# Gate and up over the blend's four PSUM banks, silu and product over 1024 columns, and an order of issue from a clock of all engines

## The chip, the cores and the metric

The kernel runs on one core of a Trainium2 chip. The metric is the device time of one execution in microseconds (us). PE is TensorE, DVE VectorE, ACT ScalarE, POOL GpSimd, SP the engine whose queue issues most DMAs.

## The reference

Eight batches of 512 tokens with 256 channels pass through a block in four parts. In outline:

```python
y   = x[b] @ W[subject].T + bias[subject]                  # a matrix per batch
q, k = silu(y @ Wq), silu(y @ Wk); v = y @ Wv              # 16 heads of 16
q, k = rotated: concat(t*cos(theta*n), t*sin(theta*n))     # 32 per head
o   = (tril(q k^T)) v                                      # causal, no softmax
x1  = x + layernorm((o @ Wo) * sigmoid(y @ G1 @ G2)) * gamma + beta

ctx   = ema(x1)                                            # along the tokens
gated = x1 * sigmoid([x1, ctx] @ Wg + bg)
mod   = 0.5 + sigmoid(gelu(x1 @ Wn1 + bn1) @ Wn2 + bn2)    # 8 traces
temporal = sum_d softmax(blend)_d * ema_d(gated * mod_d)
c  = layernorm(gelu(x1 @ Wsoma + bsoma) * sigmoid(temporal @ Wtemp + btemp) @ Wout)

# feed-forward 256 -> 1024 -> 256, weights ternary, activations to 8 bits per token
h   = silu(quant(c) @ Wgate) * (quant(c) @ Wup)
out = x1 + quant(h) @ Wdown
```

## The kernel before

The work of a batch is cut into three generators: `attention(b)`, `cond2(b)` (everything from ctx to c) and `ffn(b)`. Two more, `setup_cond2` and `setup_ffn`, prepare the weights once. Each stops at `yield` and gives back the time from which its next piece is due. A planner at the end of the function keeps a number `now`, in microseconds, and at each step takes the piece of highest rank that is due: setup first, then feed-forward, then cond2, then attention. `now` is moved on by hand-written numbers: `spent(work, then)` adds `work` and answers `now + then`. So the order in which instructions are issued is fixed when the program is built; a framework beneath it may still put an instruction of the same engine a little earlier or later, and sets the semaphores.

The parts, by the names of their PSUM tiles, for token tiles t of 128 and channel halves k or o:

- attention: pxT (transposes of x), py (y), pkq and pv per tile (`project`), then per tile pkT and pqT (transposes of the rotated k and q) and pst (running states), pe (energies, masked into et on DVE), po (output, per two tiles), pg and pgt (gate), pw (Wo). The rotation, `ktok` and `qtok`, is one POOL instruction each. After pw come a gate product og, mean and variance, a power on POOL (`rstd_a`, for four tiles at once) and the sum into x.
- cond2: px2T, the scan cT, ph (h1), pso (soma), pm (mod), pwg (gated), pc and pr (what earlier chunks carry in), ptr (the traces within a chunk, in four banks at once, each followed by four accumulations into tempT on DVE, L765), ptg, pwo, then the norm c, its quantization to cq and a DMA transpose to cqT.
- ffn: `hidden(t)` makes the gate and up of a tile in halves of 512 columns, with silu (L861) and product (L862) for each half, then the maximum hmax, the scaling and the rounding to hq. A DMA transposes hq to hqT, pd is the down projection, res its sum with x, and a DMA stores it.

PSUM has eight banks of 512 float32 columns. Four are handed out singly from the pool `ps`; the other four are one tile of the pool `ps_t` (`four_banks`), which only the blend's ptr and the setup use. Gate and up take four single banks per token tile. The next attention begins when `tail[b]` is set, after `output(1)`.

```python
            hqs[t] = hq, hstep, spent(2.1, 6.0)

        hidden(0)
        yield now[0]
        for t in range(NT):
            if t + 1 < NT:
                hidden(t + 1)
            hq, hstep, at = hqs.pop(t)
            yield at
            hqT = p2.tile([P, KI, P], BF, tag="hqT", name=f"hqT_{b}_{t}")
            nc.sync.dma_start(hqT, hq, transpose=True)
            yield spent(0.0, 4.0)
```

Of the kernel before, what the change touches and what calls it, by code (L numbers as in the profile page):

```python
# [15 lines left out]
P = 128  # L16
EPS = 1e-5
# [13 lines left out]

@with_exitstack
def adaln_attn_ffn_kernel(ctx: ExitStack, tc: tile.TileContext, a: dict, out: bass.AP):
# [13 lines left out]
    cp = ctx.enter_context(tc.tile_pool(name="const", bufs=1))  # L47
    ps = ctx.enter_context(tc.tile_pool(name="ps", bufs=4, space=bass.MemoryType.PSUM))
    ps_t = ctx.enter_context(tc.tile_pool(name="ps_t", bufs=1, space=bass.MemoryType.PSUM))
    p1 = ctx.enter_context(tc.tile_pool(name="p1", bufs=1))  # L50
    p2 = ctx.enter_context(tc.tile_pool(name="p2", bufs=2))
    p3 = ctx.enter_context(tc.tile_pool(name="p3", bufs=3))
    p4 = ctx.enter_context(tc.tile_pool(name="p4", bufs=4))
    p6 = ctx.enter_context(tc.tile_pool(name="p6", bufs=6))
# [10 lines left out]
    now = [0.0]  # L65

    def spent(work, then):

        now[0] += work
        return now[0] + then  # L70
# [5 lines left out]
    nc.vector.tensor_copy(ident_bf, ident)  # L76
    ones = cp.tile([P, P], F32, name="ones")
    nc.vector.memset(ones, 1.0)
    minus_half = cp.tile([P, 1], F32, name="minus_half")
    nc.vector.memset(minus_half, -0.5)  # L80

    causal = cp.tile([P, 64], F32, name="causal")
    for r in range(2):
        nc.gpsimd.affine_select(
            out=causal[64 * r : 64 * (r + 1), :],
            in_=ones[64 * r : 64 * (r + 1), :64],
            pattern=[[1, 64]],
            compare_op=ALU.is_ge,
            fill=0.0,
            base=0,  # L90
            channel_multiplier=-1,
        )

    own = cp.tile([P, 2, 2, HD], F32, name="own")
    nc.vector.memset(own, 0.0)
    for j in range(4):
        nc.vector.memset(own[32 * j : 32 * (j + 1), j // 2, j % 2, :], 1.0)
# [3 lines left out]
    nc.sync.dma_start(sid_t, a["sid"].rearrange("(o n) -> o n", o=1))  # L101

    def load_input(b):
        xs = p4.tile([P, NT, C], F32, tag="x", name=f"x_{b}")
        nc.sync.dma_start(xs, x[b].rearrange("(t p) c -> p t c", p=P))
        sid = nc.sync.value_load(sid_t[0:1, b : b + 1], min_val=0, max_val=NS - 1)
        wt = p1.tile([P, KC, C], F32, tag="wt", name=f"wt_{b}")
        nc.sync.dma_start(
# [4 lines left out]
        nc.sync.dma_start(bt, a["biasT"][bass.ds(sid, 1)].rearrange("s p k -> (s p) k"))  # L113
# [5 lines left out]
    def load_w(name, src, eng=nc.sync):  # L119
        rows, cols = src.shape  # L120
        t = cp.tile([P, rows // P, cols], F32, name=name)
        eng.dma_start(t, src.rearrange("(k p) n -> p k n", p=P))
        return t

    def load_row(name, src):
        t = cp.tile([P, src.shape[0]], F32, name=name)
        nc.sync.dma_start(t, src.partition_broadcast(P))
# [3 lines left out]
    nc.scalar.dma_start(theta_c, a["theta_c"])  # L131

    wkq = cp.tile([P, KC, 2, C], F32, name="wkq")
    for i, n in enumerate(("wk", "wq")):
        nc.scalar.dma_start(wkq[:, :, i, :], a[n].rearrange("(k p) n -> p k n", p=P))
    wv = load_w("wv", a["wv"], eng=nc.scalar)
# [3 lines left out]
    nc.vector.memset(g1, 0.0)  # L140
    nc.sync.dma_start(g1[:, :, :HD], a["g1"].rearrange("(k p) n -> p k n", p=P))
    g2 = cp.tile([64, C], F32, name="g2")
    nc.vector.memset(g2, 0.0)
    for u in range(2):
        nc.sync.dma_start(g2[32 * u : 32 * u + HD, :], a["g2"])
# [6 lines left out]
    nc.sync.dma_start(tau, a["taus"].partition_broadcast(P))  # L152
    blend = p1.tile([D, C], F32, tag="blend", name="blend")
    nc.sync.dma_start(blend, a["blend"])
    raws = {}

    def load_raw(n, *places):
# [3 lines left out]
            pool.tile([P, half * cols], F32, tag=tag, name=f"{n}_raw_{s}") for s, (pool, tag) in enumerate(places)  # L161
        ]
        for s, raw in enumerate(raws[n]):
            nc.sync.dma_start(
# [10 lines left out]
    for s in range(2):  # L175
        nc.sync.dma_start(w["wn2"][HN * s : HN * (s + 1), :], a["wn2T"])
        nc.sync.dma_start(w["bn1"][HN * s : HN * (s + 1), :], a["bn1"].rearrange("(p o) -> p o", o=1))
    w["bn2"] = load_row("bn2", a["bn2"])
    for n in ("bsoma", "btemp"):
        w[n] = cp.tile([P, KC], F32, name=n)  # L180
        nc.sync.dma_start(w[n], a[n])
# [13 lines left out]
    for g in range(NG):  # L195
        nc.vector.tensor_scalar(diag[:, g, :], ident, theta_c[:, g : g + 1], None, ALU.mult)
    theta = bank("theta")
    nc.tensor.matmul(theta, ones, diag.rearrange("p g n -> p (g n)"), start=True, stop=True)
# [801 lines left out]
```

## Time and profile before

| | us |
|---|---|
| median of 3 runs | 779.91 |
| lowest, highest | 776.56, 782.77 |
| the profiled execution: its own time | 779.86 |
| the profiled execution: span in the profile | 778.2 |

The profile is of one execution. In a row of its groups stand line, engine, operation, output and inputs with shapes, count, then busy time in us, mean time of one in ns, and the idle time of the engine just before with what ended it. A row of the table by stage gives a stretch `from:to` and its length, then the busy time (and count of instructions) of PE, PE's weight loads (PEld), DVE, ACT and POOL, the granted TensorE clock, the DMA share and GB/s. A row of the timeline has start, length, engine, line and operation, and in brackets the idle time before it and who released it. In the rows of digits each digit is a fortieth of the span, in tenths. A float32 matmul shows as two records. The rows of the operations that the change touches:

| row | count | busy us | mean ns |
|---|---|---|---|
| silu, L861, 512 columns | 64 | 43.2 | 687 |
| product, L862, 512 columns | 64 | 45.9 | 744 |
| hmax, L864, 1024 columns | 32 | 38.9 | 1216 |
| ktok, L296 (POOL) | 32 | 41.2 | 1286 |
| blend accumulation, L765 | 128 | 95.8 | 748 |

### The profile page before, as it was taken

How to read it: one execution, taken by the hardware profiler on the slowest of the kernel's cores; microseconds unless marked ns; L12 is line 12 of the kernel's file. 1: busy time of each engine (PE TensorE's matmuls, PEld its weight loads, DVE VectorE, ACT ScalarE, POOL GpSimd, SP SyncE). 2: the span in 40 equal slices, each digit the busy share in tenths (PEclk: the TensorE clock that was granted, in tenths of full speed). 3: DMA queues.
4: the chain of work that ended last, by engine and by line, in shares of the span. 5: the costliest groups of instructions: out<-in, count | busy, mean ns of one | idle time of the engine just before them, and what ended most of it. 6: DMA issues, size and time to landing. Idle time of an engine off the chain costs nothing.

```text
span 778.2 us, 21224 instructions
## 1 busy us (share of the span) xinstructions
PE 665.8 (86%) x9330; PEld 445.2 (57%) x9330; DVE 505.7 (65%) x1047; ACT 260.5 (33%) x480; POOL 196.7 (25%) x223
## 2 busy tenths in 40 slices
PE   2988999799888999799888999799988999795644
PEld 1566666566664666566664666466764667454312
DVE  3896355785567665775658753776658755785565
ACT  2822343243224333253234332253234333240111
POOL 3542252114301251023311152113411252110000
PEclk7969999999999999899999999999999999898756
DMA  6700000021001210022001210021000200021011
GB/s 229 231 3 3 14 2 4 15 67 56 4 16 32 56 37 3 15 63 60 4 15 21 69 35 4 16 49 48 3 16 6 69 9 3 16 55 28 1 41 54
DMA packets 61198, 28.64 MB, mean 37 GB/s; under 512 B 46346, under 2 KB 60594, under 8 KB 61106
## 3 DMA queue, kind: packets, MB, share of 16 engines
q1 hardware_dynamic: 60146, 26.50, 12.8%
q8 instruction: 73, 1.20, 0.6%
q10 hardware_dynamic: 960, 0.79, 0.3%
q14 instruction: 19, 0.16, 0.1%
HBM read 12.60 MB, written 4.19 MB: 22 GB/s over the span
## 4 chain that ended last, share of the span: by engine, by line
PE 67%; DVE 18%; issue 5%; ACT 4%; DMA 3%; POOL 3%; ACTq 0%; POOLq 0%; DVEq 0%; SPq 0%
PE pkq L273 7%; PE pwg L710 7%; PE ptr L760 5%; PE po L375 5%; PE ptg L778 4%; PE pso L682 4%; PE pv L278 3%; PE pd L885 3%; PE pe L353 3%; PE pwo L803 3%; PE pst L316 3%; PE py L261 3%; PE pw L491 2%; PE pqT L303 2%; PE pkT L303 2%
## 5 line engine op out<-in xcount | busy, mean ns | idle before, releaser
L765 DVE SCALAR_TENSOR_TENSOR tempT<-ptr,bw_c,tempT 128x512 f32<-128x512 f32 x128 | 95.8, 748 | 41.8 <-PE ptr L760 39.1
L861 ACT ACTIVATE sig<-pw_gateT,steps 128x512 f32<-128x512 f32 x64 | 43.2, 687 | 80.5 <-PE pw_gateT L858 45.9
L296 POOL TENSOR_TENSOR ktok<-sg,cs 128x512 f32<-128x512 f32 x32 | 41.2, 1286 | 108.2 <-ACT sg L280 94.9
L858 PE MATMUL pw_gateT<-w_gateT,cqT 128*128 128x512 bf16 x128 | 40.3, 398 | 31.4 <-DVE h L862 24.7
L273 PE MATMUL pkq<-wkq,yT 128*128 128x512 f32 x128 | 64.2, 622 | 0.3 <-ACT yT L262 0.3
L858 PEld LDWEIGHTS <-cqT 128*128 128x128 bf16 x256 | 25.9, 101 | 64.6 <-issue 35.9
L862 DVE SCALAR_TENSOR_TENSOR h<-pw_upT,steps,sig 128x512 f32<-128x512 f32 x64 | 45.9, 744 | 15.2 <-ACT sig L861 8.8
L375 PE MATMUL po<-et,vz 64*32 64x64 f32 x2048 | 32.0, 246 | 25.0 <-DVE et L358 15.7
L327 POOL TENSOR_TENSOR st<-total,own 128x256 f32<-128x256 f32 x56 | 41.2, 752 | 48.1 <-DVE total L337 48.1
L760 PE MATMUL ptr<-dm,gated 32*128 32x128 f32 x1024 | 40.6, 293 | 10.7 <-DVE tempT L765 10.7
L358 DVE TENSOR_TENSOR et<-pe,causal 128x512 f32<-128x512 f32 x64 | 41.8, 685 | 12.2 <-PE pe L353 12.2
L296 POOL TENSOR_TENSOR qtok<-sg,cs 128x512 f32<-128x512 f32 x32 | 40.8, 1277 | 32.7 <-PE pst L316 32.5
L885 PE MATMUL pd<-w_downT,hqT 128*128 128x256 bf16 x256 | 35.9, 288 | 14.5 <-DMA hqT<-hq 14.5
L760 PEld LDWEIGHTS ptr<-dm,gated 32*128 32x128 f32 x1024 | 33.9, 194 | 21.5 <-issue 19.5
L375 PEld LDWEIGHTS po<-et,vz 64*32 64x32 f32 x2048 | 25.0, 114 | 32.4 <-DVE et L358 19.0
L353 PE MATMUL pe<-qT,kT 32*64 32x64 f32 x2048 | 41.6, 223 | 1.3 <-ACT qT L304 0.9
L858 PE MATMUL pw_upT<-w_upT,cqT 128*128 128x512 bf16 x128 | 41.5, 408 | 1.3 <-ACT sig L861 1.3
L353 PEld LDWEIGHTS pe<-qT,kT 32*64 32x64 f32 x2048 | 35.7, 135 | 10.9 <-issue 4.1
L887 DVE SCALAR_TENSOR_TENSOR res<-pd,hstep,x 128x256 f32<-128x256 f32 x32 | 15.4, 482 | 40.7 <-PE pd L885 40.7
L885 PEld LDWEIGHTS <-hqT 128*128 128x128 bf16 x256 | 25.8, 103 | 27.5 <-DMA hqT<-hq 19.4
L405 ACT COPY aT<-po 128x256 f32<-128x256 f32 x32 | 10.5, 375 | 91.6 <-PE po L375 91.6
L864 DVE TENSOR_REDUCE hmax<-h 128x1 f32<-128x1024 f32 x32 | 38.9, 1216 | 0.3
(201 smaller groups left out, 1338.6 us busy)
## 6 DMA issues: line engine op xcount, KB each, us to landing
x<-in_x_dram SPq DMA_DIRECT2D x8, 512.0 KB, 4.3
out_dram<-res SPq DMA_DIRECT2D x32, 128.0 KB, 1.7
wt<-in_weightT_dram SPq DMA_DIRECT2D x8, 256.0 KB, 2.8
w_gateT_raw<-in_w_gateT_dram SPq DMA_DIRECT2D x2, 512.0 KB, 6.7
w_upT_raw<-in_w_upT_dram SPq DMA_DIRECT2D x2, 512.0 KB, 7.9
w_downT_raw<-in_w_downT_dram SPq DMA_DIRECT2D x2, 512.0 KB, 7.5
wgT<-in_wgT_dram SPq DMA_DIRECT2D x1, 512.0 KB, 8.7
hqT<-hq SPq DMA_TRANSPOSE x32, 2.7
```

The lines of the kernel that those rows point to most:

```text
L273: nc.tensor.matmul(pkq, yT[:, k, chunk(t)], wkq[:, k].rearrange("p e c -> p (e c)"), start=k == 0, stop=k == KC - 1)
L296: nc.gpsimd.tensor_mul(tok.rearrange("p (h e d) -> p h e d", e=2, d=HD), sgs[t][:, i].unsqueeze(2).to_broadcast([P, H, 2, HD]), cs[:, t, : ...
L353: nc.tensor.matmul(pes[e][64 * r : 64 * (r + 1), g, u, :], kT[rows, g, at], qT[rows, g, at], start=True, stop=True)
L358: nc.vector.tensor_mul(et.rearrange("p g u n -> p (g u) n"), pes[e].rearrange("p g u n -> p (g u) n"), causal.unsqueeze(1).to_broadcast([P ...
L375: nc.tensor.matmul(po[r][q : q + 32, half, u, :], *factors, start=(r, q) not in begun, stop=last)
L710: nc.tensor.matmul(pwg[:, u, :], src[:, k % KC, chunk(t + u)], w["wgT"][:, k, :], start=k == 0, stop=k == 2 * KC - 1,)
L760: nc.tensor.matmul(ptr[:, r, :, t, :], gated[rows, t, chunk(k)], dm[rows, t], start=True, stop=True)
L765: nc.vector.scalar_tensor_tensor(acc, ptr[:, :, e].rearrange("p r t n -> p r (t n)"), w["bw_c"][:, k, d + e : d + e + 1], acc, ALU.mult, A ...
L858: nc.tensor.matmul(pm, cqT[:, t, k, :], w[n][:, k, cols], start=k == 0, stop=k == KC - 1)
L861: nc.scalar.activation(sig, pgu[0], AF.Silu, scale=steps[:, 0, t : t + 1])
L862: nc.vector.scalar_tensor_tensor(h[:, cols], pgu[1], steps[:, 1, t : t + 1], sig, ALU.mult, ALU.mult)
L885: nc.tensor.matmul(pd, hqT[:, k, :], w["w_downT"][:, k, :], start=k == 0, stop=k == KI - 1)
```

## The change

Three things change together.

**The feed-forward's tiles.** `hidden(t)` becomes `inner(t)`: gate and up of a token tile are written into one `four_banks` tile, gate in two banks and up in two; one silu and one product run over 1024 columns. `sig` is one buffer of 1024 instead of two of 512. The transpose to hqT is issued right behind hq.

**The order.** Each engine is wrapped, so that every instruction issued is also put on a `Clock`: it holds for each engine the time at which it is free, for each tile when its parts were last written and read, and for each pool when a buffer comes free. Its costs are fixed formulas by engine, operation and size (with numbers of its own for some groups of matmuls). On DVE, ACT, POOL and SP an instruction may be placed in an earlier gap. A generator no longer yields a time but a function, `needs(...)`, that says from the clock when tiles and a bank will be ready; the planner takes the piece of highest rank that is ready at PE's time. The ranks stay. Setup pieces are `paced` by DVE's time.

**Pieces cut and moved.** ktok and qtok are issued within `project` (with four buffers instead of three); the tile work after it, now `turned`, has a stop before each transpose. `output(0)` comes before the last tile's transposes. dm is made right behind modt. The norm after attention takes mean, variance and power per pair of tiles. The next attention may begin when `head[b]` is set, after pg, instead of `tail[b]`; some of its pieces wait for the previous attention's `tail` or its end. More stops are set between the parts of cond2.

```diff
+class Clock:
+    MATMULS = {"ptr": 0.069, "po": 0.028, "pg": 0.125, "pgt": 0.26, "pm": 0.26}
...
+        if engine == "vector":
+            if op in ("tensor_scalar", "tensor_copy", "memset"):
+                return 0.17 + 0.00062 * n
+            return (0.1 + 0.00217 * n) if op == "tensor_tensor_scan" else 0.13 + 0.00108 * n
+        if engine == "scalar":
...
+            return load + 0.165 + 0.0009 * n + (0.2 if "accum_out" in kw else 0.0)
...
+    def needs(*aps, banks=(ps, "ps"), when=lambda: True):
+        def ready():
+            return max([clock.when(v) for v in aps] + [banks[0].free(banks[1])]) if when() else None
+
+        return ready
...
-        r = p2.tile([P, NT], F32, tag="rstd", name=name)
+        r = p2.tile([P, 2], F32, tag="rstd", name=name)
...
+            for i, n in enumerate("kq"):
+
+                toks[t, i] = tok = p4.tile([P, NG * P], F32, tag="tok", name=f"{n}tok_{b}_{t}")
+                gp.tensor_mul(
...
+        def turned(t):
+
+            yield needs(toks[t, 0])
+            turn(t, 0)
+            states(t, toks[t, 0])
+            yield needs(toks[t, 1])
+            turn(t, 1)
...
+        head[b] = True
+        yield needs(kTs[1], qTs[1])
+        energies(1, 0)
...
-        def hidden(t):
+        def inner(t):
             h = p2.tile([P, INNER], F32, tag="h", name=f"h_{b}_{t}")
-            for j in range(INNER // 512):
-                cols = slice(j * 512, (j + 1) * 512)
-                pgu = []
-                for n in ("w_gateT", "w_upT"):
-                    pm = bank(f"p{n}_{b}_{t}_{j}")
+            yield needs(cqT[:, t], banks=(ps_t, "ptr"))
+
+            pgu = four_banks(f"pgu_{b}_{t}").rearrange("p (n j) m -> p n (j m)", n=2)
+            for i, n in enumerate(("w_gateT", "w_upT")):
+                for j in range(0, INNER, 512):
                     for k in range(KC):
-                        nc.tensor.matmul(pm, cqT[:, t, k, :], w[n][:, k, cols], start=k == 0, stop=k == KC - 1)
-                    pgu.append(pm)
-                sig = p2.tile([P, 512], F32, tag="sig", name=f"sig_{b}_{t}_{j}")
-                nc.scalar.activation(sig, pgu[0], AF.Silu, scale=steps[:, 0, t : t + 1])
-                nc.vector.scalar_tensor_tensor(h[:, cols], pgu[1], steps[:, 1, t : t + 1], sig, ALU.mult, ALU.mult)
+                        te.matmul(
+                            pgu[:, i, j : j + 512],
...
+            sig = p1.tile([P, INNER], F32, tag="sig", name=f"sig_{b}_{t}")
+            ac.activation(sig, pgu[:, 0], AF.Silu, scale=steps[:, 0, t : t + 1])
+            ve.scalar_tensor_tensor(h, pgu[:, 1], steps[:, 1, t : t + 1], sig, ALU.mult, ALU.mult)
...
+            hqT = p2.tile([P, KI, P], BF, tag="hqT", name=f"hqT_{b}_{t}")
+            sy.dma_start(hqT, hq, transpose=True)
+            hqs[t] = hqT, hstep
...
-        if b < B and b in loaded and tail[b - 1]:
+        if b < B and b in loaded and head[b - 1]:
...
-        ripe = [r for r in running if running[r][0] <= now[0]]
+        now = clock.at["tensor"]
+        ready = {r: v for r, v in ((r, running[r][0]()) for r in running) if v is not None}
+        ripe = [r for r in ready if ready[r] <= now]
```

In the prediction, pgu is the gate and up tile of the changed kernel.

## The prediction

> **What bounds the kernel now.** I read the page's busy shares first, then its 40 slices, then a table by stage, then the timeline of single gaps.
>
> ```profile
> PE 665.8 (86%) x9330; PEld 445.2 (57%) x9330; DVE 505.7 (65%) x1047; ACT 260.5 (33%) x480; POOL 196.7 (25%) x223
> PE   2988999799888999799888999799988999795644
> PEclk7969999999999999899999999999999999898756
> 240.70:328.69 87.99, 80.10 (x1166) 54.57 (x1165) 57.53 (x119) 30.38 (x57) 23.47 (x25) 0.97 0.12 32
> 666.42:778.20 111.78, 70.18 (x479) 40.68 (x478) 70.28 (x142) 23.06 (x40) 6.09 (x9) 0.77 0.13 33
> ```
>
> TensorE (PE) is nearly full everywhere except at both ends. Its dips come back every 88 us: one batch. The fourth line is one whole batch: 80.1 of 87.99 us busy, so 7.9 idle. Over the five batches from 152.29 to 592.00 the idle time is 8.3, 7.9, 8.6, 7.8 and 6.5. The last line is what follows the last attention: 41.6 of 111.8 us idle. Of the 112.4 us idle in all, some 49 lie in the middle (80 to 666), 42 at the end, 21 before 80. The gaps of one batch:
>
> ```profile
> 314.36 0.35 PE L375 MATMUL po<-et,vz 64*32 64x64 f32 x16 [1.93 <-DVE et L358]
> 324.88 1.28 DVE L506 SCALAR_TENSOR_TENSOR x<-og,rstd_a,x 128x256 f32<-128x256 f32 x3 [1.24 <-POOL rstd_a L244]
> 326.47 0.75 DVE L862 SCALAR_TENSOR_TENSOR h<-pw_upT,steps,sig 128x512 f32<-128x512 f32 x1
> 327.27 0.59 PE L858 MATMUL pw_gateT<-w_gateT,cqT 128*128 128x512 bf16 x2 [3.53 <-DVE h L862]
> 743.79 1.04 PE L858 MATMUL pw_gateT<-w_gateT,cqT 128*128 128x512 bf16 x2 [6.65 <-DMA cqT<-cq]
> 771.16 3.67 PE L885 MATMUL pd<-w_downT,hqT 128*128 128x256 bf16 x16 [6.72 <-DMA hqT<-hq]
> ```
>
> The 3.53 us gap is the bank shortage: the next gate needs one of four single banks, the banks wait for the product h, and h stands on VectorE (DVE) behind a whole layer norm that itself waits 1.24 us for GpSimd's power. The last two lines are the end: nothing is left to fill PE while the last feed-forward goes round through the transposes.
>
> [...] (a pair of gate matmuls takes 1.04 us after the 6.65 us gap, 0.59 otherwise); after the 3.53 us gap the pair takes 0.59, so in mid-kernel a gap costs itself and no more. [...]
>
> **The change part by part.**
>
> *Four banks, two at once.* Per token tile, two silus (2 x 0.687) become one of 1024. No row shows that; ScalarE's (ACT) Gelu takes 474 ns for 256 elements and 687 for 512, 0.83 ns an element, so 1.11 us (the 1024-wide Sin row says 1.14). Two products (2 x 0.744) become one: 482 for 256 and 744 for 512 give 1.27. Saved: 0.25 on ACT and 0.22 on DVE per tile, 8 and 7 us over 32 tiles. Neither engine bounds, so I book nothing for it alone. What matters is that gate and up leave the four single banks, so the 3.53 us gap as such goes. What is late next: the four-bank buffer exists once, for feed-forward and blend, so gate (t+1) and the first blend wait for product t. From the last up matmul that takes about 2.0 us on a free DVE: silu ends 0.2 + 1.11 after the gate, 0.87 earlier, then 1.27, then hops. sig's single buffer adds no other wait. In the changed order 3.0 to 4.5 us of other matmuls stand between two such tiles. More on DVE is worth more than on ACT.
>
> *Transposes.* hqT is issued behind its hq, no longer at a later step. On SP's queue an input load (wt, which waits for the y matmuls) stands before hqT of tile 0 in every other batch; those matmuls end about 1 us before hq does. Output stores stand before some later hqT but wait for a down projection already past. Booked at nothing; up to 1 us a batch if wrong.
>
> *Moved POOL work.* ktok and qtok (1.29 and 1.28 us) are issued with the projection, not at their transposes, removing the releaser "PE pst" (32.5 us in the waits); dm (1.04 each) goes up to modt. POOL is 25% busy. The layer norm's rstd is taken per pair of tiles: one pow of 0.70 and a small op of 0.19 twice instead of 1.04 + 0.37, so the first pair of x no longer waits for the last pair. At the end this takes about 2 us off the way to the last transposes of x2.
>
> *Tables.* Counted in ACT's order, switches between Gelu and Silu tables go from 17 to 23, 6 x 1.28 = 8 us of ACT at 33%. The one that is near the path is silu 0 in the batches where it falls between h1 and soma; 3.5 us of pso and 1.1 of pm cover it. Booked at nothing, bound 8 us.
>
> *The order.* The order really differs, and the steady state becomes a pair of batches: in one (A) the whole feed-forward stands beside the next attention's head, in the other (B) beside the blend's head. I walked both along PE's, DVE's and POOL's order with durations from the rows above (pkq 1.72 a tile, pv 0.87, pe 1.10 a half, ptr 1.10, pso and py 3.5 and so on; DVE back to back).
> - A, first gate: after pwo's first tile come square 0.57, c 0.69, rstd 0.9, and on to cq; in the trace 307.1 to 313.6, then 2.4 to land: 9.0 us. PE has only 6.1 us to do meanwhile (half a pe, pwo, pgt, pe, three quarters of pw). Wait 3.3.
> - A, first down projection: the norm's instructions stand among hmax to hq; hqT lands 1.3 us late.
> - A, last down projection: DVE has about 38 us of work in these 42 us; hqT of tile 3 lands 3.1 us late.
> - A's blend hands the buffer over with 2.1 and 3.2 us of cover against 3.0 of DVE: 1.5 us together.
> - B: down projection of tile 2 waits 2.7, the rest about 0.8.
>
> That is 13 us in two batches, 6.5 each: the gaps are mostly replaced, not removed. But the matmuls get shorter as well: today pw is threaded into the last po stream, 314.36 to 320.92 with 1.0 before it, which costs 1.8 us more than the two apart (2.6 + 3.5); clean, a batch is 77.5 us. So 77.5 + 6.5 = 84.0; as PE arrives 1.3 us later at these waits than my rounded durations had it, 83.4. Against (592.00 - 152.29)/5 = 87.9 that is 4.5 us a batch.
>
> *Both ends.* Until 80 us PE waits 5.6 us from 53 to 81 (masks behind weight setup, then the first layer norm). The next batch's transposes, y and two projections now stand in that norm: 3 us saved, between 0 and 6. At the end, the norm by pairs saves its 2 us, and the last feed-forward is DVE's chain, 4.9 us a tile: from cqT at zero, hq of the four tiles at 7.9, 12.1, 17.7 and 23.8 (two results res stand before an hq and wait about 1 us), then 2.8 + 1.7 + 0.6 + 3 to the end: 32 against 778.2 - 743.8 = 34.4. But all four tiles of batch 6 now lie beside the last blend's head, about 28 us of DVE against 25 us today, which takes back 2 to 3. Net 2 us.
>
> *Sum.* 4.5 us x 6.7 batches (80 to 672) = 30, and 3 + 2: 35 us off the span of 778.2, 743. Outside the span lie 779.86 - 778.2 = 1.7 us: 745. The profiled execution and the median of the runs (779.91) agree, so no correction.
>
> **The rivals.**
> - *Nearly full filling.* The walk has DVE strictly behind; if the waits shrink to 1.5 us a batch, it is 79 us, 8.9 x 6.7 + 5 = 65 off: 715. For it: DVE is 57.5 of 88 us busy on average. Against it: it is dense where the feed-forward is.
> - *The waits move and don't shrink.* As many gaps as today plus the DVE backlog, 8.5 us a batch: 86.0, 1.9 x 6.7 + 5 = 18 off: 762. If the threading of po and pw isn't won either, 775 to 780: the change then doesn't do what its order says. For it: the durations on which an order rests are fixed numbers in both kernels, and today's order leaves 8 us as well.
> - *Slower: the one four-bank buffer.* Five handovers a batch (four tiles, then the first blend). If DVE is behind at each by 1 us more than walked, 5 us a batch, the gain of 4.5 + 0.7 is gone; from there it decides. At 2 us more: (10 - 5.2) x 6.7 = 32 us slower, 812. For it: today DVE was 3.5 us behind at exactly such a product. Against: 3.0 to 4.5 us of cover at each, and DVE spared 0.22 us a tile.
>
> **How the numbers follow.** My forecast, 728 to 760, has 0.60; nearly full filling 0.13; moved waits (760 to 772) 0.11; within 1%, which is about what a measurement of this kernel can tell from no change, 0.08; slower 0.08. So faster by over 1% is 0.84. The range 716 to 777 leaves out half of the full filling and the slower end: under 2 in 10. The bounds of unknown terms are inside it: tables up to +8, SP up to +7, waits per batch 1.5 to 8.5.
>
> **What would show it.** Right: batches of about 83 us; no PE gap released by the product of 0.5 us or more except at the first gate; the longest mid-kernel PE gaps at the first gate (cqT) and at down projections (hqT), 1 to 3 us; the silu near 1.1, the product near 1.27; a last stage from the last cqT of 32 us. Wrong: gaps of over 2 us before gates or blends, released by DVE, in every batch (the buffer), or batches of 86 us and more, or of 80 and less.

## The result and the profile after

The changed kernel takes 784.07 us (median of 20 runs, 779.88 to 792.12), the kernel before 781.53 beside it (20 runs, 776.56 to 790.6): 1.0034 of before, 95% interval 1.001 to 1.0058. (Ratios leave out slow executions, over 1.5% above the fastest of the same kernel; medians count all.) The forecast was 745. The profiled execution of the changed kernel took 789.42 us (span 787.7), some 5 us above its own median, so the two traces lie 9.5 us apart where the medians lie 2.5 apart.

In the changed kernel nearly all instructions carry the line of the engine wrapper (L167), so groups are told apart by their tiles; pgu is gate and up. First the page's busy shares of PE and DVE, PE's slices and granted clock:

```profile
PE 661.9 (84%) x9313; PEld 443.1 (56%) x9330; DVE 511.4 (65%) x1015; ACT 254.0 (32%) x452; POOL 213.4 (27%) x239
...
PE   2789898889988899999898798999988899685654
...
PEclk7977899989999999999999999999999999896756
```

PE's dips are still there and the idle time has grown (125.8 us against 112.4). From the table by stage, a whole pair of batches twice (the order repeats every two), then what follows the last attention's output projection:

```profile
267.76:441.19 173.43, 157.35 (x2324) 107.47 (x2329) 116.95 (x231) 61.17 (x108) 51.40 (x54) 0.96 0.14 32
441.19:612.50 171.31, 154.77 (x2323) 105.75 (x2329) 116.87 (x231) 61.18 (x108) 51.39 (x54) 0.98 0.12 28
674.10:787.70 113.60, 67.01 (x354) 37.25 (x355) 70.08 (x139) 20.28 (x32) 6.73 (x11) 0.72 0.13 33
```

A batch takes (173.43 + 171.31)/4 = 86.2 us, of it 78.0 busy and 8.2 idle; before it took 87.9. The last row is 113.6 us long; before, from the same matmul to the end, it was 106. PE's waits over the whole run (us, times, longest), the kernel before:

```profile
PE pw_gateT L858 <- DVE h L862: 24.7, 7, 3.5
PE po L375 <- DVE et L358: 15.7, 9, 1.9
PE pd L885 <- DMA hqT<-hq: 14.5, 3, 6.7
```

and the changed kernel, then the same view of its pair 267.7 to 441.19 alone:

```profile
PE pd L167 <- DMA hqT<-hq: 19.9, 11, 4.4
PE pgu L167 <- DMA cqT<-cq: 19.9, 5, 6.7
...
PE pqT L167 <- DVE res L167: 11.3, 6, 2.7
PE pgu L167 <- DVE h L167: 7.6, 3, 2.5
```
```profile
PE pqT L167 <- DVE res L167: 6.4, 3, 2.7
PE pd L167 <- DMA hqT<-hq: 4.8, 2, 3.1
PE po L167 <- issue: 3.7, 2, 2.3
PE ptr L167 <- DVE tempT L167: 1.6, 3, 1.0
```

The wait of the gate for the product is gone from the middle, as forecast; its last three cases are in the last feed-forward, and the last blend waits 2.0 us for a product once (at 707.6). In its place stand many waits of 0.4 to 3 us. (Of the 6.4 us, 2.66 end just where the window begins.)

At the head, VectorE in the changed kernel, then before:

```profile
65.97 1.29 DVE L167 TENSOR_TENSOR et<-pe,causal 128x512 f32<-128x512 f32 x2 [1.25 <-PE pe L167]
75.35 0.16 DVE L167 TENSOR_SCALAR wstep<-pwsum 128x1 f32<-128x1 f32 x1 [8.10 <-PE pwsum L167]
...
75.75 1.42 DVE L167 TENSOR_SCALAR w_downT_raw<-w_downT_raw,winv 128x1024 f32<-128x1024 f32 x2
...
79.67 0.75 DVE L167 SCALAR_TENSOR_TENSOR og<-gate,pw 128x256 f32<-128x256 f32 x2
```
```profile
70.60 0.75 DVE L496 SCALAR_TENSOR_TENSOR og<-gate,pw 128x256 f32<-128x256 f32 x2 [5.06 <-issue]
```

VectorE stands 8.1 us for a sum over w_down (pwsum) that PE issues only behind the po stream, then does that weight's setup, and only then the first norm (og): 9 us later than before. The first blend's last ptg ends at 142.2 instead of 126.8. Not all of this belongs to the change. last_single (below) issues the same instructions in the same order up to the last batch; in its profiled execution og begins at 77.09 and that ptg ends at 137.7. The granted clock up to 160 us is 0.94 there and 0.88 here: the eight y matmuls that begin at 75.18 take 5.38 us here and 3.68 there. So about 4.5 of the 15 us (142.2 against 137.7), by my estimate from these two executions, go with the granted clock of this one.

At the end, PE's timeline:

```profile
750.54 0.61 PE L167 MATMUL pgu<-w_gateT,cqT 128*128 128x512 bf16 x1 [6.65 <-DMA cqT<-cq]
...
756.66 1.87 PE L167 MATMUL pgu<-w_gateT,cqT 128*128 128x512 bf16 x4 [2.52 <-DVE h L167]
...
762.75 1.86 PE L167 MATMUL pgu<-w_gateT,cqT 128*128 128x512 bf16 x4 [2.52 <-DVE h L167]
...
776.19 1.89 PE L167 MATMUL pd<-w_downT,hqT 128*128 128x256 bf16 x8 [2.41 <-DMA hqT<-hq]
782.49 1.89 PE L167 MATMUL pd<-w_downT,hqT 128*128 128x256 bf16 x8 [4.42 <-DMA hqT<-hq]
```

The gates start 6.1 to 6.8 us apart: eight matmuls, silu, product, in series on the one buffer. Of the 6.1 us from 756.66 to 762.75, the eight matmuls take 3.6, at a granted clock of 0.50, and the handover 2.52; from 750.5 to the end the granted clock is 0.59. From the last cqT to the end it takes 37.2 us; before it was 34.4.

### The profile page after: what moved, and what is told of

Same layout as the page of the kernel before. It is cut to its first block, busy times and chain, and to the rows that moved or that the text cites. A ratio compares the mean times of both kernels' runs of the same rounds, so it can differ in the third digit from the quotient of the medians.

```text
span 787.7 us, 21069 instructions
## 1 busy us (share of the span) xinstructions
PE 661.9 (84%) x9313; PEld 443.1 (56%) x9330; DVE 511.4 (65%) x1015; ACT 254.0 (32%) x452; POOL 213.4 (27%) x239
## 4 chain that ended last, share of the span: by engine, by line
PE 51%; DVE 16%; DMA 5%; issue 4%; ACT 3%; POOL 1%; POOLq 0%; DVEq 0%; ACTq 0%; SPq 0%
PE pgu L167 6%; PE pwg L167 6%; PE pkq L167 6%; DVE tempT L167 5%; PE ptr L167 4%; DMA hqT<-hq 3%; PE ptg L167 3%; PE pso L167 3%; PE pd L167 3%; PE pwo L167 3%; PE pv L167 2%; DVE h L167 2%; PE po L167 2%; DVE c L167 2%; PE pr L167 2%
## 5 line engine op out<-in xcount | busy, mean ns | idle before, releaser
L167 DVE SCALAR_TENSOR_TENSOR tempT<-ptr,bw_c,tempT 128x512 f32<-128x512 f32 x128 | 96.0, 750 | 36.4 <-PE ptr L167 33.1
L167 POOL TENSOR_TENSOR ktok<-sg,cs 128x512 f32<-128x512 f32 x32 | 41.3, 1292 | 171.1 <-ACT sg L167 157.7
L167 PE MATMUL pkq<-wkq,yT 128*128 128x512 f32 x128 | 71.0, 678 | 0.3 <-DMA bg<-in_bg_dram 0.3
L167 DVE SCALAR_TENSOR_TENSOR h<-pgu,steps,sig 128x1024 f32<-128x1024 f32 x32 | 41.0, 1280 | 42.6 <-ACT sig L167 42.6
L167 POOL TENSOR_TENSOR st<-total,own 128x256 f32<-128x256 f32 x56 | 44.5, 807 | 87.9 <-DVE total L167 87.4
L167 ACT ACTIVATE sig<-pgu,steps 128x1024 f32<-128x1024 f32 x32 | 35.7, 1115 | 90.4 <-PE pgu L167 90.4
L167 PEld LDWEIGHTS <-cqT 128*128 128x128 bf16 x256 | 26.0, 105 | 62.4 <-DMA cqT<-cq 22.2
L167 PE MATMUL pgu<-w_gateT,cqT 128*128 128x512 bf16 x111 | 35.2, 425 | 28.7 <-DMA cqT<-cq 19.9
L167 PE MATMUL ptr<-dm,gated 32*128 32x128 f32 x1024 | 44.0, 298 | 17.4 <-DVE tempT L167 15.2
L167 PE MATMUL pd<-w_downT,hqT 128*128 128x256 bf16 x256 | 37.6, 296 | 20.6 <-DMA hqT<-hq 19.9
L167 PEld LDWEIGHTS ptr<-dm,gated 32*128 32x128 f32 x1024 | 36.4, 198 | 28.5 <-issue 21.4
L167 DVE TENSOR_TENSOR et<-pe,causal 128x512 f32<-128x512 f32 x64 | 41.6, 681 | 7.2 <-PE pe L167 7.2
L167 POOL TENSOR_TENSOR qtok<-sg,cs 128x512 f32<-128x512 f32 x32 | 46.0, 1437 | 0.0
L167 PEld LDWEIGHTS <-hqT 128*128 128x128 bf16 x256 | 25.5, 105 | 31.7 <-DMA hqT<-hq 24.2
L167 PEld LDWEIGHTS pe<-qT,kT 32*64 32x64 f32 x2048 | 35.8, 136 | 12.3 <-issue 8.4
L167 PE MATMUL pe<-qT,kT 32*64 32x64 f32 x2048 | 41.4, 225 | 0.1
L167 ACT ACTIVATE sg<-pkq 128x512 f32<-128x512 f32 x32 | 19.1, 598 | 65.4 <-PE pkq L167 65.4
L167 ACT ACT_TABLE_LOAD x28 | 35.9, 1283 | 12.7 <-PE pkq L167 7.6
L167 DVE TENSOR_REDUCE hmax<-h 128x1 f32<-128x1024 f32 x32 | 38.7, 1210 | 0.3
L167 PE MATMUL py<-xT,wt 128*128 128x512 f32 x64 | 34.5, 673 | 3.6 <-ACT xT L167 3.6
L167 PE MATMUL pgu<-w_upT,cqT 128*128 128x512 bf16 x128 | 37.0, 415 | 0.0
L167 PEld LDWEIGHTS pkq<-wkq,yT 128*128 128x128 f32 x128 | 25.5, 217 | 20.3 <-issue 17.2
```

The lines of the kernel that those rows point to most:

```text
L167: made = issue(*args, **kw)
```

## The experiments

Ratios are to the kernel before, run beside each on the same chip, with their 95% intervals; the changed kernel's is 1.0034. The theories that the expectations name: 1, the middle's waits are VectorE's backlog, as the new order packs its work too densely; 2, the last feed-forward goes in series through the one buffer; 3, the pacing of the weight setup delays the first norm; 4, which batch of a pair comes last decides the end. Three more came up on the way: 5, the clock packs the feed-forward so closely that it uses up whatever VectorE is relieved of; 6, the clock's PE runs ahead of the chip's; 7, VectorE's instructions get longer beside GpSimd's. An order is "made anew" where the clock is told of an edit, and "kept" where it counts the old instruction.

### One half of the change at a time

banks_only: the kernel before, with (in outline)

```diff
-                for n in ("w_gateT", "w_upT"): pm = bank(...)     # two silus, two products
+            pgu = four_banks(f"pgu_{b}_{t}")                       # one silu, one product
```

> The kernel before with its own planner and order; gate and up go into the four-bank tile, one silu and one product over 1024 columns; no clock. Theory 1 (the new order packs VectorE's feed-forward and norm work too densely, and that is why 4 us a batch did not come): the buffer alone takes away the 3.5 us gap before a gate in each batch but adds handovers to the blend, and costs at the end, where a silu cannot start before the up matmuls are done (3 x 2 us): 772 to 785 us. Rival A (the buffer brings the gain and the new order gives it back): 750 to 765. Rival B (the buffer itself is the loss and the order the gain): 795 to 815, with waits of 2 us and more for the product before gates or blends in every batch.

order_only: the changed kernel, with the opposite edit in `inner`.

> The changed kernel's clock, order and moved pieces; gate and up in halves of 512 in four single banks, two silus and two products per tile, as before. Theory 1 (VectorE dense in the new order): the batch stays at 86 to 88 us, since VectorE has 0.2 us more per tile, and the end is 4 to 6 us shorter than in the changed kernel because silu follows its own half: 777 to 787 us. Rival B (the shared buffer is what holds the batch at 86): batches of 83, 755 to 765. Rival A (buffer gains, order loses): 800 and more.

Measured: banks_only 797.29 us, 1.0156 of before (1.01 to 1.0212); order_only 826.53, 1.0563 (1.052 to 1.0607). Both are slower than the two together. PE's waits, banks_only first, then order_only:

```profile
PE px2T L658 <- DVE x L506: 27.2, 9, 3.8
PE pd L888 <- DMA hqT<-hq: 21.4, 10, 4.4
```
```profile
PE pd L167 <- DMA hqT<-hq: 48.0, 10, 7.5
PE pw_gateT L167 <- DMA cqT<-cq: 34.0, 8, 7.0
```

With the old order the 3.5 us gap before a gate only moves on, to the transposes of x2 that wait for the norm: 24.7 us became 27.2. With the new order and single banks a batch takes 92 us. Neither came out as theory 1 had it: banks_only fell in the range of rival B, for which the buffer is the loss, and order_only in that of rival A, for which the order is. A reading that fits both is that the order needs the single banks that the buffer sets free, and the buffer needs the order. What is shown is that each half alone loses in the one form tried; in order_only the clock also made its order anew, and the order alone can move this kernel by tens of us (below).

### Where the next attention begins

```diff
-        if b < B and b in loaded and head[b - 1]:
+        if b < B and b in loaded and tail[b - 1]:
```

> The changed kernel, but the next attention begins where it did before the change, at the previous one's tail and not at its head. Theory (the early start is what makes the long and short batches alternate, and fills PE): batches of equal length, about 87 to 89 us, total 788 to 800. Rival (alternation is itself a loss, because in every second batch the whole feed-forward stands beside one other stage): batches of 83 to 85, total 765 to 775.

Measured: 791.4 us, 1.0107 (1.0072 to 1.0142), with batches of nearly equal length (84 to 91 us between the transposes of x2). The early start is a gain of 6 to 7 us, with the order that came with it.

### Head and end

setup_early, in `paced`:

```diff
-        return lambda: max([clock.when(v) for v in aps] + [clock.at["vector"] - 1.0])
+        return lambda: max([clock.when(v) for v in aps], default=0.0)
```

> The changed kernel, but the pieces of the weight setup come as soon as their inputs are there, not paced by VectorE's time. Theory 3 (pacing puts the weight setup of w_down between the first attention's output and its norm, and the first wpo ends 10 us later than before): first transposes of x2 back at 78 to 80 us instead of 87, total 6 to 9 us less, 775 to 778. Rival (PE has other work then, the next attention's head, so the time is not lost but taken later): total within 2 us of the changed kernel, with the following batch's stages no earlier than in it.

Measured: 773.41 us, 0.9872 (0.9828 to 0.9916). Its norm begins without the setup ahead of it:

```profile
72.74 0.75 DVE L167 SCALAR_TENSOR_TENSOR og<-gate,pw 128x256 f32<-128x256 f32 x2 [2.12 <-issue]
```

PE is idle 10.1 us from 30 to 160 instead of 18.5, and the first blend's last ptg ends at 130.0. But the edit also turned the pair over: the long intervals now follow the other batches, and from the last output projection to the end it takes 101 us, not 113.6, since less of batch 6's feed-forward lies beside the last blend. flip1 turns the pair over with the setup left paced:

```diff
-        if b < B and b in loaded and head[b - 1]:
+        if b < B and b in loaded and (tail if b == 1 else head)[b - 1]:
```

> The changed kernel, weight setup paced as in it; only the second attention (batch 1) begins at the tail of the first one, all later ones at the head as in the changed kernel. This turns the alternation over: the batches with the long interval become the odd ones, as in the run with unpaced setup, and the last blend no longer has the sixth batch's feed-forward beside it. Theory 4 (of the 11 us that unpaced setup won, the larger part is which batch comes last): 107 us from the last attention's output projection to the end become 100 to 103, and the total is 774 to 779. Rival (the setup's place itself is the loss): the end may be shorter, but the later start of batch 1 costs as much: 782 to 788.

Measured: 780.04 us, 0.9957 (0.9934 to 0.998). The end shortened to 104 us; the head was hardly better than in the changed kernel (16.5 us idle from 30 to 160). So, as far as one run of each can tell, roughly half of what setup_early won (0.8 of 1.6%) is which of the two batches comes last, and the other half is the head.

last_single: single banks in the last batch alone (`if b == B - 1:` with the old code).

> The changed kernel, only the last batch's gate and up in halves in four single banks. Theory 2 (at the end PE, silu and product go in series on the one four-bank buffer, 2.5 us of wait and a halved clock per tile): from the last cqT to the end 31 to 33 us instead of 37, total 4 to 6 us less than the changed kernel, 778 to 780. Rival (the end is VectorE's chain of about 5 us a tile, whatever the banks): 36 to 37 us, total within 1 us of the changed kernel or slower by 1 from VectorE's 0.2 us a tile.

Measured: 780.01 us, 0.9971 (0.9922 to 1.002): 4 us less than the changed kernel, though the two intervals touch. Its last feed-forward on PE:

```profile
746.17 0.63 PE L167 MATMUL pw_gateT<-w_gateT,cqT 128*128 128x512 bf16 x1 [7.05 <-DMA cqT<-cq]
...
771.78 3.34 PE L167 MATMUL pd<-w_downT,hqT 128*128 128x256 bf16 x16 [6.79 <-DMA hqT<-hq]
```

No gate waits for a product here, and from the last cqT to the end it takes 32.3 us instead of 37.2. That is the shortest of its kind. In the other traces with single banks at the end and the same work per tile it takes 34.4 (the kernel before), 34.6 (order_only), 34.9 (best) and 35.3 us (early_last); in those with the one buffer, 36.3 to 38.3. So the one buffer made the end longer, by about 3 us rather than 5. VectorE's chain counts at least as much: hmax_same and hmax_short (below), with the one buffer and one shorter VectorE instruction a tile, take 32.1 and 32.0 us.

> The changed kernel with both edits: weight setup not paced, and the last batch's gate and up in single banks. If head and end are independent losses they add up: 773.4 - 4 = 769. If what single banks saved was chance of order: 773 as without them. If the last feed-forward is then bound by VectorE: 771 to 773.

early_last, both edits: 772.66 us, 0.9814 (0.9767 to 0.9861). Its median is 0.8 us under that of setup_early, and the intervals of the two ratios overlap. That the two gains add up is not shown, and the 769 was not reached.

### VectorE's amount, or the chain of one tile

hmax_short and hmax_same shorten one VectorE instruction a tile:

```diff
-            ve.tensor_reduce(hmax, h, AX.X, ALU.max, apply_absolute_value=True)
+            ve.tensor_reduce(hmax, h[:, :8], AX.X, ALU.max, apply_absolute_value=True)      # hmax_short
+            nc.vector.tensor_reduce(hmax, h[:, :8], AX.X, ALU.max, ...)                     # hmax_same
+            clock.account("vector", "tensor_reduce", (hmax, h), {})
```

> The changed kernel, with the maximum of h taken over 8 of its 1024 columns (so the scaling of h, and the output, are other numbers): VectorE has about 1.0 us less per token tile, 4 us a batch, and nothing else moves in the chip; the clock counts the shorter instruction and may shift the order a little. Theory 1 (the waits at cqT, hqT, res and tempT are VectorE's backlog): a pair of batches takes 164 to 167 us instead of 172 to 173, the end is 4 us shorter, total 750 to 762. Rival (the waits are fixed latencies of transposes, hops and the order, VectorE's amount of work hardly matters): pair 170 and more, total 776 to 782.

> As hmax_short (maximum over 8 of 1024 columns, another scaling of h), but the clock counts the instruction at its full size, so the order of issue is the changed kernel's own to the last instruction: VectorE has about 1.0 us less per token tile and nothing else differs. Theory 1 (the middle's waits are VectorE's backlog; in hmax_short the clock used the time up by packing tiles closer): a pair of batches takes 164 to 168 us instead of 172, total 755 to 765. Rival (waits are set by fixed chains, not by VectorE's amount): pair 170 to 172, total 774 to 780.

Measured: hmax_short 778.82 us, 0.9954 (0.9927 to 0.9981); hmax_same 763.35, 0.9725 (0.9668 to 0.9782). The same relief of the chip is worth 21 us where the clock is not told of it and 5 where it is: with the shorter cost the clock makes another order. Between the second and the seventh transposes of x2, two batches take 174 to 175 us in hmax_short and 164 to 168 in hmax_same, against 166 to 174 in the changed kernel.

scale_act takes another VectorE instruction away and puts it on ScalarE, the clock not told:

```diff
-            ve.tensor_scalar(h, h, hinv, MAGIC, ALU.mult, ALU.add)
+            nc.scalar.activation(h, h, AF.Identity, bias=magic, scale=hinv)
+            clock.account("vector", "tensor_scalar", (h, h), {})
```

> The changed kernel, the scaling of h (0.75 us a tile on VectorE) done by ScalarE (about 1.1 us), with the clock still counting it on VectorE, so that the order stays. VectorE has 27 us less in all and the scaling no longer meets GpSimd; each tile's own chain gets about 0.5 us longer. Theory 1 (relief of VectorE pays where GpSimd doesn't get more): hmax_same won 0.65 us per us of VectorE taken away, so 12 to 18 us less, minus the longer chain at the end (2): 768 to 774. Rival (the single chain of a tile decides, not VectorE's total): 784 to 790.

Measured: 802.86 us, 1.0221 (1.0188 to 1.0254), 19 us slower than the changed kernel. VectorE is busy 489.7 us there, 484.5 in hmax_same, 511.4 in the changed kernel: it lost much the same work both times, with opposite results. What differs is the chain of one tile: from the end of the product to the end of hq it takes 4.07 us on average in the changed kernel, 2.81 in hmax_same, 4.96 in scale_act. PE's waits for hqT, 19.9 us in the changed kernel, follow it (hmax_same, then scale_act):

```profile
PE pd L167 <- DMA hqT<-hq: 10.4, 8, 3.3
```
```profile
PE pd L167 <- DMA hqT<-hq: 34.3, 11, 4.4
```

So theory 1 fell in the form it was given. With the changed kernel's order, it is the length of a tile's own chain that the middle pays for, not VectorE's total. Two things stay open: scale_act is slower than even the rival expected (784 to 790), and it makes ScalarE 36.7 us busier (290.7), which was not tested apart.

### res off VectorE, and GpSimd's part

res_on_act, and res_same with the clock counting the old instruction:

```diff
-            ve.scalar_tensor_tensor(res, pd, hstep, x2[:, t, :], ALU.mult, ALU.add)
+            ac.activation(res, pd, AF.Copy, scale=hstep)
+            gp.tensor_add(res, res, x2[:, t, :])
```

> The changed kernel, the sum res is made by a scaled copy from PSUM on ScalarE and an addition on GpSimd, so that a down projection's bank is not held by VectorE's queue. Theory (the six waits of the q transposes for res, 11.3 us together, are a loss of their own): they vanish, 6 to 11 us less than the changed kernel, 773 to 778. Rival (the same VectorE backlog then shows at the next wait: hqT, cqT or tempT): 781 to 786, with the sum of PE's waits unchanged within 3 us.

> The changed kernel with res on ScalarE and GpSimd as in res_on_act, but the clock still counts it as VectorE's instruction, so that the order stays the changed kernel's own. Theory 5 (relief of VectorE is worth its time where the order is kept, and the clock spends it where the order is made anew): 32 x 0.48 us = 15 us less on VectorE, of it 7 to 11 us off the total, 772 to 777. Rival (res is no part of the backlog that PE waits for; order doesn't matter here): as res_on_act, 781 to 784.

Measured: 782.63 us, 0.9998 (0.9975 to 1.0021), and 788.35, 1.0083 (1.0057 to 1.0109). The waits for res vanish in both, and others take their place (projections that wait for `total`, 6.6 us in each; hqT 31.0 us in res_same). The expected gain of res_same turned into a loss, though the order was kept. 15.2 us of res left VectorE, but it is only 4.4 us less busy (507.0). Two rows of VectorE tell a part of why, before, after and in res_same (minimum, median and maximum in ns; the last block has sums and means):

```profile
L868 DVE TENSOR_SCALAR h<-h,h_inv x32: 752/754/756, 157.6 to 768.6; 128x1024 f32<-128x1024 f32 x32
```
```profile
L167 DVE TENSOR_SCALAR h<-h,h_inv x32: 752/753/1340, 167.1 to 777.9; 128x1024 f32<-128x1024 f32 x32
L167 DVE TENSOR_SCALAR hq<-h x32: 677/694/1420, 167.9 to 779.0; 128x1024 bf16<-128x1024 f32 x32
```
```profile
L167 DVE TENSOR_SCALAR h<-h,h_inv 128x1024 f32<-128x1024 f32 x32 | 29.7, 929 | 0.0
L167 DVE TENSOR_SCALAR hq<-h 128x1024 bf16<-128x1024 f32 x32 | 27.8, 867 | 0.6
```

In the changed kernel every long one lies beside a GpSimd instruction (last section). pool_light takes the rotations off GpSimd: `nc.scalar.copy` stands in place of `gp.tensor_mul`, so the rotation itself is left out, and the clock counts the old instruction.

> The changed kernel, the 64 rotations (1.3 to 1.4 us each on GpSimd) replaced by copies on ScalarE without the cosines and sines (the rotation is left out), counted by the clock as before so that the order stays. GpSimd has 87 us less, VectorE's instructions meet it less often. Theory 7 (VectorE's longer instructions beside GpSimd are a part of the loss): scaling and rounding of h back near 0.75 and 0.69, VectorE 4 to 6 us less busy, total 4 to 10 us less, 774 to 780. Rival (contention falls where PE does not wait): VectorE less busy, total 782 to 786.

Measured: 780.56 us, 0.9946 (0.9925 to 0.9966), 3.5 us or, by the ratios, 0.9% less than the changed kernel. Scaling and rounding average 0.78 and 0.71 us. But the gain does not lie where these stand. The first product of a feed-forward begins at 154.3 us, in the changed kernel at 164.1 and in last_single at 159.6. From that product to the end of the last transposes of x2, pool_light and the changed kernel both take 520.1 us, and PE waits longer for hqT (27.1 us against 19.9). So what was won came before the first feed-forward; that scaling and rounding beside GpSimd cost the kernel time, theory 7, is not shown. (ScalarE, busy 286.6 us instead of 254.0 with the copies, may hide a gain.)

### The order alone

dve_dear and pe_dear change nothing but the clock's costs:

```diff
             work = self.cost(engine, op, outs[0], on_chip, kw)
+            work *= 1.15 if engine == "vector" else 1.0      # dve_dear
+            work *= 1.1 if engine == "tensor" else 1.0       # pe_dear
```

> The changed kernel's work to the last instruction; only the clock counts every VectorE instruction 15% longer, which puts more other matmuls between two feed-forward tiles of the batches beside the next attention (transposes of x2 and a projection, 4 us, between the first two, where there were the soma matmuls). Theory 5 (the clock packs the feed-forward too close for the VectorE that is there): a batch 84 to 85 us, total 772 to 778. Rival (the clock's costs are near the chip's, and any error in them costs): 788 to 800.

> The changed kernel's work; only the clock counts every matmul 10% longer, which brings its PE to the busy time that the profile shows (about 660 us). Theory 6 (the clock's PE runs ahead of the chip's, so pieces are called ripe in another succession than they become so): 772 to 778. Rival (waits of the changed kernel do not come from these costs): 782 to 786.

Measured: dve_dear 816.57 us, 1.0448 (1.0395 to 1.0502); pe_dear 771.56, 0.9877 (0.9842 to 0.9913). The same work in another order lies 45 us apart, more than the 35 us that were forecast for the change. dve_dear went against theory 5. In pe_dear a tile's chain is longer than in the changed kernel (4.79 us from product to hq), PE waits longer for hqT (32.1 us against 19.9), and it is faster all the same: no q transpose waits for res, and the stops in the po stream come to 5.0 us instead of 12.4. So with another order the chain of a tile alone does not decide. Why an order 10% dearer in matmuls is the better one is not settled; a single trial in each direction can't tell a better cost from a lucky order. The same holds for order_only, start_at_tail, setup_early, flip1, hmax_short and res_on_act, in which the clock also made its order anew: their ratios are of the edit together with the order that it drew.

### Versions put together

No edit here is new: early_last_res is early_last with res_on_act's two lines, early_last_res_same the same with res_same's, best is early_last with pe_dear's.

> The changed kernel with three edits: setup not paced, last batch's gate and up in single banks, res on ScalarE and GpSimd. If the three are independent: 772.7 - 1.5 = 771. If res on VectorE costs more in this order (waits of the q transposes for res 11.5 us there): 763 to 767. If the additions on GpSimd get in the way of rstd and the rotations: 774 to 778.

> The three edits of early_last_res, with the order kept as it is with res on VectorE. If keeping the order is what pays: 2 to 6 us less than early_last_res, 758 to 762. If the new order was as good: 762 to 766. If early_last_res had drawn a lucky order: 768 to 772.

> The changed kernel with setup not paced, the last batch's gate and up in single banks, and the clock's matmuls counted 10% longer. If the gains add up (11 + 1 to 4 + 12): 757 to 762. If setup_early and pe_dear won by the same thing (which batches alternate, and what lies beside the last blend): 768 to 772.

Measured: early_last_res 763.85 us, 0.9744 (0.9689 to 0.98); early_last_res_same 769.31, 0.982 (0.9777 to 0.9862); best 775.79, 0.9864 (0.9827 to 0.9901). The first beats both kernels by 2.6% and more. best, above both of its forecasts, did not add up: pe_dear and setup_early win about as much alone as together with single banks at the end. Part of early_last_res is thus the order that it happened to draw: the same chip work with the order kept is 5 us slower by the medians, though the intervals just meet.

## Why the prediction was wrong, point by point

The forecast was 35 us less; the medians came out 2.5 more, the profiled executions 9.5 more. The 45 us between forecast and profile split into about 19 in the middle (2.8 us a batch times 6.7), 9 at the end (2 less were forecast, 7.5 more were measured from the last output projection on), and the rest, some 17, at the head; of these about 4.5 go with the granted clock of the profiled execution.

- *Sizes of the operations: right.* Silu 1.11 (measured 1115 ns), product 1.27 (1280 ns), a table load 1.28 (1283 ns in both traces); no gap before a gate released by the product except at the very end.
- *The handover of the buffer: mis-sized.* "About 2.0 us on a free DVE", because silu was to start after the gate. In all 32 tiles of the trace silu starts 0.04 us or more after the last up matmul, never before, so the handover is 2.52. In the middle other matmuls cover it; at the end nothing does, and it is paid three times in the last feed-forward.
- *The middle: the step that failed is the list of waits.* Its waits for cqT, hqT and ptr came to 12.7 us a pair; the pair shown has 6.4 of these (hqT 4.8, ptr 1.6). Not on the list were the q transposes that wait for a bank held by pd until res (3.7 us in the pair) and the stops within the po stream (3.7), which the kernel before has too (9.5 us over the run). So 8.2 idle for 6.5; 78.0 busy for 77.5; and the 0.6 us credited for PE's later arrival was not there. The 77.5 did not follow from its own working: 80.1 less the 1.8 us of the threading is 78.3, near what was measured. "The waits move and don't shrink", the rival at 86.0 us a batch, is what the middle did (86.2).
- *The price of a gap: misread.* "In mid-kernel a gap costs itself and no more" was read off the one pair of matmuls after the 3.53 us gap at 327.27. In that same trace the granted clock is 0.50 from 328.5 to 331.9, and eight transposes take nearly twice their time:

```profile
72.07 1.04 PE L254 MATMUL pxT<-ident,x 128*128 128x128 f32 x8
...
328.49 1.91 PE L254 MATMUL pxT<-ident,x 128*128 128x128 f32 x8
```

Six of the seven gaps of 3.53 us are followed within 2 us by such a stretch of 3.4 us. Gaps of 1.68, 1.93 and 2.31 us are followed by one too (at 474.0, 314.4 and 386.0), while the 3.53 us gap that ends at 592.9 and two of 1.93 us (405.0 and 493.3) are not: the length of a gap alone does not tell, in this trace, whether one follows. A batch of the kernel before thus has 6.6 us at half clock, one of the changed kernel 5.1: a price that the sum left out, paid by both kernels.

- *POOL's moved work: "booked at nothing" is not refuted.* I had taken GpSimd's 25% busy as cover and not asked what VectorE runs beside it: scaling and rounding take 5.7 us longer in all than before (27.1 and 24.8 us for 24.1 and 22.1). That this cost PE anything, pool_light does not show.
- *The head: the step failed in sign.* I put the next batch's transposes and projections into the gap and booked 3 us as saved, "between 0 and 6". `paced` was in the diff, and I did not follow what it does: w_down's setup, with its sum behind PE's po stream, comes ahead of the first norm. The first blend ended 15 us later, 11 in last_single's execution of the same order.
- *The end: failed.* I expected 32 us from the last cqT on VectorE's chain of 4.9 us a tile; the loop through the one buffer is 6.1. That stretch took 37.2 us, and with single banks 32.3 to 35.3 in five traces. And "takes back 2 to 3" for batch 6's feed-forward beside the last blend was too low: turning the pair over shortens the stretch after the last output projection from 113.6 to 104 us.
- *The rival on the slow side: not it.* No wait for a product decided in the middle. At the end the buffer did: 2.0 us before the last blend and three times 2.52 in the last feed-forward.

## What to carry to other kernels

When an order of issue is made from estimated costs, an edit has two effects, the one on the chip and the one on the order; keep the order fixed and measure the first alone, or a gain of 21 us reads as one of 5. A shared buffer and the order that fills around it belong together: each half of this change alone, in the one form tried, lost 1.6 and 5.6%. Price the ends of a pipelined program by themselves, with the setup, and ask which of two alternating batches comes last; here head and end took back all that the middle had won. And look at the granted clock after a gap, not only at the first matmul behind it: here 3.4 us at 0.50 followed six of the seven gaps of 3.53 us.

## What the runs showed of the hardware

VectorE's scaling of h and its rounding to hq take 0.75 and 0.69 us alone. In the changed kernel 7 of 32 scalings overlap a GpSimd instruction and take 1.2 us on average, up to 1.34; 12 of 32 roundings do and take 0.9 on average, up to 1.42. Each of the ten long ones (1.14 us and more) overlaps a rotation or dm, the work that moved; one scaling beside dm keeps its 0.75, and eight roundings beside modt, rstd_a or st keep 0.68 to 0.70. In the kernel before none of the 32 scalings met a GpSimd instruction, and the 7 roundings that did, all beside modt, kept their 0.69, so its trace did not show it; overlap alone does not lengthen them. The product (1.28 us, 4 of 32 overlapping), hmax (1.21, 6 of 32) and the blend's accumulations (0.75, 27 of 128) are as long beside GpSimd as alone. GpSimd's rotations get longer too: the 9 of 64 that overlap a scaling or a rounding take 1.54 us on average, the other 55 1.34, but up to 2.19, so these two do not account for all of it. GpSimd's timeline in the changed kernel, the first qtok beside scaling and rounding, the second without:

```profile
262.61 1.73 POOL L167 TENSOR_TENSOR qtok<-sg,cs 128x512 f32<-128x512 f32 x1
...
273.63 1.27 POOL L167 TENSOR_TENSOR qtok<-sg,cs 128x512 f32<-128x512 f32 x1
```

So the rotations and dm, where they were moved to, lengthened scaling and rounding on VectorE in 10 of the 11 cases in which they met them. No run here tells why these lengthen and hmax does not.

The stops inside the po stream, up to 2.3 us after about a hundred short matmuls, released by nothing that the profile shows, occur 9 times in both kernels (9.5 and 12.4 us). No run here tells what they are.
